# Moving the ordering and turning of the last part of w eleven places later, and regrouping the engines that copy it

## The chip, the cores and the metric

One core of a Trainium2 chip (trn2). The metric is the device time of one execution in microseconds (us), the median of several. The program runs on one core only. Profiles are of single executions; their span is some 1.8 us shorter than the device time of the same execution.

## The reference, cut to what matters

```python
# inputs: r_inputs (B=4096, F=32, D=64) float32, W (P=496, 64, 64) float32, P = F (F-1) / 2
idx_i, idx_j = np.triu_indices(F, k=1)
vi = inputs[:, idx_i, :]
vj = inputs[:, idx_j, :]
vidots = jnp.einsum('bpd,pde->bpe', vi, W)
return vidots * vj                       # (4096, 496, 64) float32: 520 MB
```

Each of 496 pairs of fields has its own 64 x 64 matrix. The output is large (520 MB), the inputs small (42 MB together).

## The kernel before

A tile is 128 rows of the batch; there are 32. A tile takes 46 steps (up to 16 pairs each), in five output parts of 6, 7, 9, 10 and 14 steps; one transfer writes one part of one tile. The first three tiles are interleaved part by part, because w comes in only while they run: part 1 of tiles 0, 1, 2 (steps 0 to 17), part 2 (18 to 38), part 3 (39 to 65), part 4 (66 to 95), part 5. Each part of w (w0 to w3, 128 pairs each, w3 112) is loaded, brought into another order by four copies ("order", `rp<-raw`), turned by TensorE and copied out of PSUM ("turn", `ptw`, `wT`). w2 and w3 share one raw buffer, so w3 can be loaded only when the last copy of w2 has read it.

```python
    tpool = ctx.enter_context(tc.tile_pool(name="tpool", bufs=4))    # rp and tmp share these four
    opool = ctx.enter_context(tc.tile_pool(name="opool", bufs=3))    # output parts
...
        pool, tag = ((opool, "ot"), (opool, "ot"), (const, "w3"), (const, "w3"))[c]
...
    def order_w(c: int, k: int, copy):
        r = wrows[c][1] - wrows[c][0]
        rp = tpool.tile([P, EU, 2, D], F32, tag="tmp", name=f"rp_{c}_{k}")
        src = raw[c][:r, :].rearrange("p (d h e) -> p e h d", h=2, d=D)
        copy(rp[:r], src[:, k * EU : (k + 1) * EU])
        return rp
...
    for c, orders, turns in (                       # at which step of the interleaved schedule
        (1, (2, 4, 8, 10), (4, 7, 12, 15)),
        (2, (17, 22, 27, 32), (19, 24, 29, 34)),
        (3, (43, 44, 45, 46), (48, 50, 52, 54)),
    ):
...
    no_aside = range(41, 55)
...
                rps[c, k] = order_w(c, k, p if c > 1 and k % 2 else v)   # p GpSimd, v VectorE
                if (c, k) == (2, NU - 1):
                    load_w(3, nc.scalar)
...
        if i in aside and c0 == 0 and s not in no_aside:     # "aside": ScalarE and GpSimd
            tmp = tpool.tile([P, CH, 2, E2], F32, tag="tmp", name=f"tmp_{s}")
            nc.scalar.copy(tmp, src)
            nc.gpsimd.tensor_mul(dst, tmp, xj)
        else:
            nc.vector.tensor_mul(dst, src, xj)
```

The order in which an engine runs its instructions is not quite the written one: in the trace of this kernel VectorE's two copies of w3, written for steps 43 and 45, run right after its product of step 39. In the lines of a trace, `ot<-ps,xs` is a product on VectorE, `ot<-tmp,xs` one on GpSimd, `out_dram<-ot` an output.

Of the kernel before, what the change touches and what calls it, by code (L numbers as in the profile page):

```python
# [12 lines left out]
def kernel(  # L13
# [52 lines left out]
    def rows_of(dram: bass.AP, blk: int) -> bass.AP:  # L66
        return dram[blk * NB * P : (blk + 1) * NB * P]

    def new_x(blk: int):

        xs[blk] = xpool.tile([P, 1 + NB * F, D], F32, tag="xs", name=f"xs_{blk}")
        nc.gpsimd.memset(xs[blk][:, 0, :], 0.0)  # L72

    def load_x(blk: int, eng, k0: int = 0, k1: int = NB):
        src = rows_of(x, blk).rearrange("(p k) f d -> p (k f) d", k=NB)
        eng.dma_start(out=xs[blk][:, 1 + k0 * F : 1 + k1 * F, :], in_=src[:, k0 * F : k1 * F, :])  # L76
# [7 lines left out]
    def load_w(c: int, eng=nc.sync):  # L84

        a, b = wrows[c]
        pool, tag = ((opool, "ot"), (opool, "ot"), (const, "w3"), (const, "w3"))[c]
        raw[c] = pool.tile([P, D * D], F32, tag=tag, name=f"raw_{c}")
        eng.dma_start(out=raw[c][: b - a, :], in_=wflat[a:b])
# [8 lines that stand above are left out]
    def turn_w(c: int, k: int, rp, copy):  # L98
        r = wrows[c][1] - wrows[c][0]
        if c not in wT:  # L100
            wT[c] = const.tile([P, r, E2], F32, tag=f"w{c}", name=f"wT_{c}")
        pt = psum.tile([P, EU, P], F32, tag="ps", name=f"ptw_{c}_{k}")
        for n in range(EU):
            nc.tensor.transpose(  # L104
                pt[:, n, :r], rp[:r, n].rearrange("p h d -> p (h d)"), ident[:r, :r]
            )
        copy(wT[c][:, :, k * EU : (k + 1) * EU], pt[:, :, :r].rearrange("p e r -> p r e"))  # L107

    def turn_x(blk: int, k: int, q: int, copy):

        pt = psum.tile([P, RUN, P], F32, tag="ps", name=f"ptx_{blk}_{k}_{q}")
        for n in range(RUN):
            s = k * F + q * RUN + n
            nc.tensor.transpose(  # L114
                pt[:, n, :], xs[blk][:, s : s + 2, :].rearrange("p f d -> p (f d)"), ident
            )
        xT = xtpool.tile([P, RUN, P], F32, tag="xT", name=f"xT_{blk}_{k}_{q}")
        copy(xT, pt)  # L118
        return xT
# [31 lines left out]
    for c, orders, turns in (  # L151
        (1, (2, 4, 8, 10), (4, 7, 12, 15)),
        (2, (17, 22, 27, 32), (19, 24, 29, 34)),
        (3, (43, 44, 45, 46), (48, 50, 52, 54)),
    ):
        for k in range(NU):
            due.setdefault(orders[k], []).append(("order", c, k))
            due.setdefault(turns[k], []).append(("turn", c, k))
    no_aside = range(41, 55)
    LATE = 6  # L160
    loads = {place[blk * NB, LATE]: blk + 1 for blk in range(2, NBLK - 1)}
    loads[place[LEAD, LATE]] = 2
# [10 lines left out]
    v, p, a = nc.vector.tensor_copy, nc.gpsimd.tensor_copy, nc.scalar.copy  # L173
    xT, rps = {}, {}
# [8 lines left out]
    for s, (t, st) in enumerate(sched):  # L183
        blk, kt = divmod(t, NB)
        g, i, c0, m = steps[st]
        if s in loads:
            new_x(loads[s])
            load_x(loads[s], nc.scalar)
        for what, *args in due.get(s, ()):
            if what == "x":  # L190
                xT[tuple(args)] = turn_x(*args, a)
            elif what == "turn":
                turn_w(*args, rps.pop(tuple(args)), a)
            else:
                c, k = args
                rps[c, k] = order_w(c, k, p if c > 1 and k % 2 else v)
                if (c, k) == (2, NU - 1):
                    load_w(3, nc.scalar)

        base, end = groups[g]  # L200
        pa = p0[i] + c0
        if pa == base:
            ots[t] = opool.tile([P, cap, D], F32, tag="ot", name=f"ot_{t}_{g}")
        ot = ots[t]
        ps = psum.tile([P, 2, CH, E2], F32, tag="ps", name=f"ps_{s}")
        for c, (lo, hi) in enumerate(wrows):
            lo, hi = max(pa, lo), min(pa + m, hi)
            if lo < hi:
                for h in range(2):
                    n = i + 1 - h  # L210
                    nc.tensor.matmul(  # L211
                        ps[:, h, lo - pa : hi - pa, :],
                        xT[blk, kt, n // RUN][h * D : (h + 1) * D, n % RUN, :],
                        wT[c][h * D : (h + 1) * D, lo - wrows[c][0] : hi - wrows[c][0], :],
                        start=True,
                        stop=True,
                    )
        o = pa - base
        j = 1 + kt * F + i + 1 + c0
        dst = ot[:, o : o + m, :].rearrange("p m (h e) -> p m h e", h=2)  # L220
        src = ps[:, :, :m, :].rearrange("p h m e -> p m h e")
        xj = xs[blk][:, j : j + m, :].rearrange("p m (h e) -> p m h e", h=2)
        if i in aside and c0 == 0 and s not in no_aside:
# [6 lines that stand above are left out]
        ends = (p0[2], end) if s < NS and (t, g) == (0, 0) else (end,)  # L230
        if pa + m in ends:
            n0 = p0[2] if len(ends) > 1 and pa + m == end else base
            nc.sync.dma_start(  # L233
                out=rows_of(out, blk).rearrange("(p k) n d -> p k n d", k=NB)[:, kt, n0 : pa + m, :],
                in_=ot[:, n0 - base : pa + m - base, :],
            )
# [27 lines left out]
```

## Time and profile before

| | before |
|---|---|
| device time, median of 3 (range) | 1362.47 us (1362.38 to 1362.98) |
| span of the profiled run | 1360.9 us |
| share of the span busy: PE, DVE, ACT, POOL | 87%, 71%, 27%, 39% |
| mean of the transfers over the span | 414 GB/s |
| the same from 80 to 105 us | 281 GB/s |
| the same from 300 to 600 us | 421 GB/s |

Read the last two rows together. In all but its start the kernel moves about 421 GB/s; between 80 and 105 us it moves a third less, and what is not moved there has to be moved later. The lines behind the table are in the prediction.

### The profile page before, as it was taken

What the parts mean: (1) busy time and instruction counts of PE and PEld (TensorE: products, weight loads), DVE (VectorE), ACT (ScalarE), POOL (GpSimd) and SP (SyncE); (2) the same over time, 40 slices, a digit from 0 to 9 for tenths busy, and PEclk for the clock granted to TensorE, in tenths of its full rate; (3) what the DMA queues carried; (4) which work ended last, traced back from release to release, by engine and by line L of the source; (5) the groups of instructions that cost most, each with busy time, mean ns of one, the idle gap of its engine ahead of it and who ended that gap; (6) DMA issues with size and microseconds to landing.
All of it is one profiled execution on the core that took longest, in us unless ns stands there. A gap on an engine that the chain in (4) does not pass through costs nothing.

```text
span 1360.9 us, 17864 instructions
## 1 busy us (share of the span) xinstructions
PE 1178.6 (87%) x7424; PEld 690.8 (51%) x7424; DVE 960.9 (71%) x1263; ACT 371.5 (27%) x366; POOL 534.4 (39%) x247
## 2 busy tenths in 40 slices
PE   6969898889889897988879989898887989988994
PEld 4546554545455454554445555455554545545552
DVE  4778776757777676776767767577775768767774
ACT  3422222222222222322322222222222322223321
POOL 1634233443333443434434334443344434344431
PEclk9989998989989899998989989899998999989997
DMA  9979999999999999999999999999999999999997
GB/s 380 371 320 432 420 428 433 430 426 426 420 415 423 429 416 414 422 416 424 425 412 417 420 415 426 416 419 412 427 410 421 426 413 424 409 431 421 419 419 318
DMA packets 26273, 562.92 MB, mean 414 GB/s; under 512 B 2912, under 2 KB 2912, under 8 KB 3040
## 3 DMA queue, kind: packets, MB, share of 16 engines
q1 hardware_dynamic: 24048, 530.59, 91.9%
q10 hardware_dynamic: 2144, 31.20, 5.5%
q8 instruction: 58, 0.95, 0.3%
q14 instruction: 23, 0.19, 0.0%
HBM read 41.68 MB, written 520.09 MB: 413 GB/s over the span
## 4 chain that ended last, share of the span: by engine, by line
DMA 49%; PE 27%; DVE 17%; POOL 2%; issue 2%; ACT 0%; DVEq 0%; SPq 0%; POOLq 0%; ACTq 0%
DMA out_dram<-ot 47%; PE ps L211 22%; DVE ot L228 17%; PE ptx L114 4%; POOL ot L226 2%; DMA raw<-in_L_rec_W_dram 2%; PE ptw L104 1%; DVE rp L95 0%; ACT tmp L225 0%; POOL rp L95 0%; DVEq L228 0%; ACT wT L107 0%; SPq L76 0%; SPq L233 0%; POOLq L226 0%
## 5 line engine op out<-in xcount | busy, mean ns | idle before, releaser
L228 DVE TENSOR_TENSOR ot<-ps,xs 128x1024 f32<-128x1024 f32 (+15 forms) x1251 | 945.2, 809 | 361.0 <-DMA out_dram<-ot 179.5
L211 PE MATMUL ps<-wT,xT 64*128 64x512 f32 (+13 forms) x6272 | 1033.7, 473 | 131.6 <-DVE ot L228 120.3
L211 PEld LDWEIGHTS ps<-wT,xT 64*128 64x128 f32 x6272 | 563.8, 197 | 566.6 <-DVE ot L228 305.3
L226 POOL TENSOR_TENSOR ot<-tmp,xs 128x1024 f32<-128x1024 f32 x221 | 522.2, 2363 | 644.5 <-ACT tmp L225 456.3
L225 ACT COPY tmp<-ps 128x1024 f32<-128x1024 f32 x221 | 223.9, 1013 | 505.6 <-PE ps L211 462.2
L118 ACT COPY xT<-ptx 128x1024 f32<-128x1024 f32 x128 | 129.6, 1013 | 440.2 <-PE ptx L114 440.2
L114 PE MATMUL ptx<-ident,xs 128*128 128x128 f32 x1024 | 141.2, 281 | 28.9 <-DVE ot L228 20.1
L114 PEld LDWEIGHTS ptx<-ident,xs 128*128 128x128 f32 x1024 | 111.0, 142 | 74.5 <-issue 44.3
L72 POOL MEMSET xs<- 128x64 f32 x16 | 2.4, 152 | 148.2 <-DVE ot L228 148.2
L95 DVE COPY rp<-raw 128x1024 f32<-128x1024 f32 (+1 forms) x11 | 15.1, 1410 | 18.1 <-DMA raw<-in_L_rec_W_dram 18.1
L104 PE MATMUL ptw<-ident,rp 128*128 128x128 f32 (+1 forms) x128 | 18.9, 303 | 3.9 <-DVE rp L95 3.9
L104 PEld LDWEIGHTS ptw<-ident,rp 128*128 128x128 f32 (+1 forms) x128 | 16.1, 158 | 11.0 <-DVE rp L95 5.0
L107 ACT COPY wT<-ptw 128x1024 f32<-128x1024 f32 (+1 forms) x15 | 14.8, 985 | 17.6 <-PE ptw L104 15.2
L95 POOL COPY rp<-raw 128x1024 f32<-128x1024 f32 (+1 forms) x4 | 9.4, 2350 | 6.7 <-DMA raw<-in_L_rec_W_dram 6.7
L107 DVE COPY wT<-ptw 128x1024 f32<-128x1024 f32 x1 | 1.2, 1225 | 3.5 <-PE ptw L104 3.5
L95 ACT COPY rp<-raw 128x1024 f32<-128x1024 f32 x1 | 2.0, 1964 | 1.8 <-DMA raw<-in_L_rec_W_dram 1.8
L118 ACT ACT_TABLE_LOAD x1 | 1.3, 1283 | 0.7 <-PEq L251 0.7
masks.py:197 POOL MEMSET ident<- 128x128 f32 x1 | 0.2, 205 | 0.3 <-POOLq L251 0.3
masks.py:199 POOL TENSOR_SCALAR_AFFINE_SELECT ident<-ident 128x128 f32<-128x128 f32 x1 | 0.3, 294 | 0.0
L251 POOL MEMSET const-float32-0.0<- 128x1 f32 x1 | 0.1, 99 | 0.2 <-issue 0.2
L251 POOL MEMSET const-bfloat16-1.0<- 128x1 bf16 x1 | 0.1, 102 | 0.0
L251 POOL MEMSET const-uint8-127<- 128x1 uint8 x1 | 0.1, 102 | 0.0
(1 smaller groups left out, 0.1 us busy)
## 6 DMA issues: line engine op xcount, KB each, us to landing
out_dram<-ot SPq DMA_DIRECT2D x64, 3360.0 KB, 16.2
out_dram<-ot SPq DMA_DIRECT2D x32, 3168.0 KB, 15.2
out_dram<-ot SPq DMA_DIRECT2D x32, 3104.0 KB, 17.0
out_dram<-ot SPq DMA_DIRECT2D x31, 2880.0 KB, 16.4
xs<-in_r_inputs_dram ACTq DMA_DIRECT2D x14, 2048.0 KB, 16.6
raw<-in_L_rec_W_dram SPq DMA_DIRECT2D x3, 2048.0 KB, 14.5
xs<-in_r_inputs_dram SPq DMA_DIRECT2D x2, 1024.0 KB, 11.1
xs<-in_r_inputs_dram SPq DMA_DIRECT2D x1, 2048.0 KB, 24.9
```

The lines of the kernel that those rows point to most:

```text
L72: nc.gpsimd.memset(xs[blk][:, 0, :], 0.0)
L95: copy(rp[:r], src[:, k * EU : (k + 1) * EU])
L104: nc.tensor.transpose(pt[:, n, :r], rp[:r, n].rearrange("p h d -> p (h d)"), ident[:r, :r])
L107: copy(wT[c][:, :, k * EU : (k + 1) * EU], pt[:, :, :r].rearrange("p e r -> p r e"))
L114: nc.tensor.transpose(pt[:, n, :], xs[blk][:, s : s + 2, :].rearrange("p f d -> p (f d)"), ident)
L118: copy(xT, pt)
L211: nc.tensor.matmul(ps[:, h, lo - pa : hi - pa, :], xT[blk, kt, n // RUN][h * D : (h + 1) * D, n % RUN, :], wT[c][h * D : (h + 1) * D, lo - ...
L225: nc.scalar.copy(tmp, src)
L226: nc.gpsimd.tensor_mul(dst, tmp, xj)
L228: nc.vector.tensor_mul(dst, src, xj)
L251: nc = _bacc.Bacc("TRN2", target_bir_lowering=False, num_devices=1)
```

## The change

Its intent: w3 is needed for the first time at step 75, but its ordering stood at step 43, where VectorE and GpSimd met a load that had not landed. The ordering and turning go eleven places later, and half of w3's copies go from GpSimd to ScalarE. The new expression also sends w2's two even copies from VectorE to GpSimd.

```diff
-        (3, (43, 44, 45, 46), (48, 50, 52, 54)),
+        (3, (54, 54, 55, 55), (57, 60, 63, 66)),
...
-    no_aside = range(41, 55)
+    no_aside = range(52, 67)
...
-                rps[c, k] = order_w(c, k, p if c > 1 and k % 2 else v)
+                rps[c, k] = order_w(c, k, (v, v, p, v)[c] if k % 2 == 0 else (v, v, p, a)[c])
```

## The prediction

> **What bounds the kernel now.** I read the page first (which engine is full, and where in the span), then the chain of waits around the odd slice, then a table of windows cut at the edges that the chain gave, then each engine's timeline there.
>
> The page: the DMA row gives the busy share of the 16 engines in each fortieth of the span (34 us), GB/s what they moved.
>
> ```profile
> span 1360.9 us, 17864 instructions
> ...
> DMA  9979999999999999999999999999999999999997
> GB/s 380 371 320 432 420 428 433 430 426 426 420 415 423 429 416 414 422 416 424 425 412 417 420 415 426 416 419 412 427 410 421 426 413 424 409 431 421 419 419 318
> ```
>
> The transfers are full from the fourth slice on, at about 420 GB/s; the kernel is bound by writing its 520 MB. Only the first three slices and the last are below that. So the change can earn nothing but DMA idle time in the start, and the third slice (68 to 102 us, 320 GB/s) is the worst. The chain of waits between 40 and 130 us (start, length, what):
>
> ```profile
> 51.63 2.41 POOL ot L226
> 54.05 1.94 POOL rp L95
> 55.98 0.02 issue
> 56.01 16.33 DMA raw<-in_L_rec_W_dram
> ...
> 73.37 5.04 DVE rp L95
> 78.41 0.61 DVE ot L228
> 79.02 0.04 issue
> 79.06 1.97 PE ptx L114 x8
> ```
>
> The last part of w (w3) can be loaded only when GpSimd's last ordering copy of w2 has left the shared buffer (55.98); it lands at 72.34; then VectorE copies it for six microseconds; then TensorE goes on. Windows (time, length, busy time per engine, PE clock, DMA share, GB/s):
>
> ```profile
> 65.80:80.20 14.40, 2.92 (x22) 2.21 (x19) 7.77 (x5) 0.33 (x1) 7.68 (x3) 0.73 1.00 425
> 80.20:84.90 4.70, 4.70 (x28) 3.23 (x28) 3.78 (x5) 1.44 (x2) 0.04 (x1) 0.74 0.02 3
> 84.90:92.90 8.00, 8.00 (x64) 5.60 (x62) 5.75 (x6) 3.40 (x5) 0.00 (x0) 1.00 0.95 406
> 92.90:95.60 2.70, 2.70 (x22) 1.55 (x20) 2.20 (x4) 0.74 (x2) 0.00 (x0) 1.00 0.00 0
> 80.00:105.00 25.00, 25.00 (x177) 16.36 (x175) 19.13 (x26) 10.47 (x11) 7.33 (x4) 0.95 0.66 281
> 300.00:600.00 300.00, 266.87 (x1682) 155.36 (x1680) 216.40 (x287) 81.96 (x81) 121.59 (x55) 0.95 0.99 421
> ```
>
> While the engines stand still the DMA still has work, until 80.2; then it is idle for 4.7 us, writes one output, and is idle again for 2.7 us. The output issues in SyncE's timeline agree: none between 65.81 and 84.94, the next at 95.61. The engines' timelines of the copies concerned, VectorE's, GpSimd's and ScalarE's (start, length, instructions merged, idle time before and what ended it):
>
> ```profile
> 50.77 1.05 DVE L95 COPY rp<-raw 128x1024 f32<-128x1024 f32 x1
> 62.87 2.75 DVE L228 TENSOR_TENSOR ot<-ps,xs 128x640 f32<-128x640 f32 x3 [1.19 <-PE ps L211]
> 72.43 5.98 DVE L95 COPY rp<-raw 112x1024 f32<-112x1024 f32 x2 [6.81 <-DMA raw<-in_L_rec_W_dram]
> ```
>
> ```profile
> 72.46 2.77 POOL L95 COPY rp<-raw 112x1024 f32<-112x1024 f32 x1 [6.67 <-DMA raw<-in_L_rec_W_dram]
> ```
>
> ```profile
> 11.31 1.96 ACT L95 COPY rp<-raw 128x1024 f32<-128x1024 f32 x1 [1.78 <-DMA raw<-in_L_rec_W_dram]
> ```
>
> An ordering copy costs VectorE 1.05 us alone, but 2.99 each (5.98 for two) beside a copy on GpSimd; GpSimd 1.99 alone (at 42.20 and 53.99) and 2.7 here; ScalarE 1.96. VectorE's 6.81 us of waiting and 5.98 of copying are the hole in which no product was written out.
>
> **What the Trainium skill says.** "SBUF — State Buffer", section "SBUF: two separate sides": VectorE in a two-port mode and GpSimd take an exclusive lock on a shared port pair for a whole instruction; ScalarE has ports of its own. The 5.98 us for two copies against 2 x 1.05 agrees in direction. "ScalarE: Activation LUTs", section "What ACT_TABLE_LOAD costs": an activation with immediate scale and bias takes 186 ns + 0.833 ns per element, 1.04 us for 1024. The copies out of PSUM agree (1013 ns); the strided ordering copy took 1.96, and I use that. "DMA: Bandwidth & Descriptors", section "Issuing engines are not separate DMA queues": transfers issued from different engines interleave on the same 16 engines. The w3 load agrees: 1.79 MB took 16.33 us beside the outputs, 110 GB/s of the 425 moved. So an earlier order to read w3 is not to be had cheaply, a later use is.
>
> **The change part by part.** Steps 39 to 65 of the interleaved schedule are the third of five output parts for tiles 0, 1, 2 (nine steps each); step 66 on is the fourth part.
>
> First, the four w3 orderings leave steps 43 to 46 for 54 and 55, and the turns leave 48 to 54 for 57 to 66. The turned w3 holds pairs from 384 on and is first read at step 75 (the tenth step of the fourth part), so nothing waits for it that did not. Removed from VectorE at 65.6 us: 6.81 + 5.98 = 12.8 us. TensorE stood from 67.6 (four PSUM buffers full) to 79.06: 11.5 us. That is the most the engines can gain.
>
> What the DMA makes of it: between 80 and 105 us it moved 281 x 25 = 7.0 MB. At the 421 GB/s of the full stages that is 16.7 us. So 8.3 us is to be had: 4.7 + 2.7 idle, and the rest because a transfer alone in the queue ran at 406. It is had in full if the third part's outputs are issued before the queue runs dry. Estimate: tile 0 has about 40 matmuls at 6.43/40 us (the 40 before the hole) = 6.4 us and one turn of x (1.0): issued at about 65.8 + 7.4 = 73.2. Tile 1 carries two ordering copies on VectorE and one product more: seven products outside the aside 5.5 us (from the means by form), + 1.2 + 2 x 1.05 = 8.8: 82. Tile 2 has all nine products on VectorE, 8.0: 90. The queue, at 3.24 MB per output and 421 GB/s (7.7 us), would be empty at 80.2, 87.9, 95.6. Margins of 7, 6 and 6 us: no idle. Gain 8.3.
>
> Second, half of the w3 copies go to ScalarE: 2 x 1.96 us on an engine that is 27% busy, and VectorE's two return from 2.99 to about 1.05. This lies inside the margin.
>
> Third, and not in the words of the change: the new expression sends all four w2 copies to GpSimd; two of them (steps 17 and 27) were VectorE's. GpSimd gets 2 x 1.99 = 4.0 us, VectorE loses 2.1, which earns nothing as TensorE is 100% busy from 20 to 66 us. GpSimd was idle 3.6 us before 39.52 and 1.6 us before 48.15, which would take most of it. What doesn't fit pushes the aside products, the w3 load and the outputs of the second part. Estimated cost 0 to 2.4 us; I take 0.7.
>
> Fourth, the steps that may not use the aside become 52 to 66 instead of 41 to 54: four products instead of three are moved to VectorE, +1.2 us, counted above.
>
> Sum: 1362.5 - 8.3 + 0.7 = 1354.9, say 1355.
>
> **Rivals.** (a) The wait stays in another place: the copies run in an order near, but not equal to, the written one (the w3 copies of step 43 ran right after the product of step 39). If VectorE still meets them before the load lands, only their cost shrinks, and the hole ends about 4 us earlier: 1358. Eleven places are about 8 us of work, and the load was 6.8 late, so this is close, but the 6 us margin covers a small rest. ScalarE, too, may now stand before w3 and hold up turns of x. (b) GpSimd becomes the bound from 40 to 62 us, being busy 13.7 of 18 us from 38 to 56: everything 2.4 us later or more, 1357 to 1358. (c) The transfers hide it all: 1362. Against it: from 130 us on the queue is never empty, so idle time in the start is never made good, and its removal is passed on in full. (d) The engines' whole 11.5 us is won: 1351. Against it: the queue has no more than 8.3 to give here.
>
> **Range and chances.** The centre is 1355; a full gain with no loss on GpSimd, or a little DMA idle before 56 us saved too, gives 1353; (a) and (b) together about 1360. I put 8 in 10 between 1353 and 1360. Two per cent is 27 us, three times all the idle at issue, so within 2% is nearly certain: faster 0.01, same 0.98, slower 0.01.
>
> **What would show it.** Right: the third slice rises from 320 towards 420 GB/s, no window of DMA share 0 between 80 and 96, the first output of the third part issued at 72 to 78 instead of 84.94, the VectorE copies of w3 near 1.05 us, the span shorter by the DMA idle removed, and slices four to 39 unchanged. Wrong: outputs of the second part issued over 2 us later (then the GpSimd term is too small), a new wait of ScalarE or VectorE for the load of w3 that outlasts the queue, or the same hole at another place.

## The result, and the profile after

| | before | changed |
|---|---|---|
| device time, median (range) | 1362.62 us (1362.38 to 1362.98), 4 runs | 1355.01 us (1354.39 to 1355.39), 4 runs |
| ratio, 95% interval | | 0.9943 (0.9926 to 0.9961) |
| span of the profiled run | 1360.9 us | 1353.3 us |
| transfers, 80 to 105 us | 281 GB/s | 402 GB/s |
| outputs of part 3 issued, tiles 0, 1, 2 | 84.94, 95.61, 101.68 us | 71.24, 85.44, 94.85 us |

A ratio is the mean time of one kernel's fast runs over that of the other's of the same rounds, so it is not quite the ratio of the medians. The change makes the kernel 7.6 us faster by the medians, which is 0.6% and well within 2%.

The page of the changed kernel: the span, the transfers' busy share and what they moved, in fortieths of the span.

```profile
span 1353.3 us, 17856 instructions
...
DMA  9999999999999999999999999999999999999997
GB/s 386 370 426 408 424 427 431 428 432 431 418 414 419 433 412 418 422 413 426 428 407 422 417 425 410 423 421 407 425 410 426 419 422 427 401 432 428 415 417 319
```

The third slice went from 320 to 426 GB/s, and its busy digit from 7 to 9. The second slice (370) is still low. The fourth fell from 432 to 408 (the low share near 103 us, shown below, lies in it); those after it are about as before. So the time was won in the third slice.

The chain of waits of the changed kernel, from 56 us on:

```profile
56.12 2.42 POOL ot L226
58.54 0.02 issue
58.55 16.29 DMA out_dram<-ot
...
75.64 2.61 DVE rp L95
78.25 0.60 DVE ot L228
78.85 0.95 DVE rp L95
```

The load of w3 is gone from it. At the same place there is now a transfer in the other direction: the output issued at 58.55 (part 2 of tile 1), whose buffer part 3 of tile 1 needs. It is split into sixteen shares; the first landed at 72.75 us, the last at 74.84, and VectorE began at 74.96. VectorE's timeline there, then ScalarE's and GpSimd's:

```profile
69.55 1.62 DVE L228 TENSOR_TENSOR ot<-ps,xs 128x1024 f32<-128x1024 f32 x2 [0.30 <-PE ps L211]
74.96 0.76 DVE L228 TENSOR_TENSOR ot<-ps,xs 128x576 f32<-128x576 f32 x1 [3.79 <-DMA out_dram<-ot]
75.64 2.61 DVE L95 COPY rp<-raw 112x1024 f32<-112x1024 f32 x1
78.16 0.69 DVE L228 TENSOR_TENSOR ot<-ps,xs 128x512 f32<-128x512 f32 x1
78.76 1.04 DVE L95 COPY rp<-raw 112x1024 f32<-112x1024 f32 x1
```

```profile
72.13 1.93 ACT L95 COPY rp<-raw 112x1024 f32<-112x1024 f32 x1
77.38 1.98 ACT L95 COPY rp<-raw 112x1024 f32<-112x1024 f32 x1 [3.33 <-POOL ot L226]
```

```profile
75.00 2.35 POOL L226 TENSOR_TENSOR ot<-tmp,xs 128x1024 f32<-128x1024 f32 x1 [4.40 <-DMA out_dram<-ot]
```

Three things are to be seen. VectorE waits 3.79 us, no longer for w3 but for the output buffer. Its two copies took 2.61 and 1.04 us: the first began at 75.64, while GpSimd was in a product from 75.00 to 77.35, and ended 0.9 us after that product. This is what the Trainium skill, "SBUF — State Buffer", section "SBUF: two separate sides", describes: the shared port pair is held for a whole instruction, and the other engine waits until it is free. The trace fits: elsewhere in this trace VectorE's ordering copies take 1.02 to 1.07 us, and 77.35 + 1.05 = 78.40, 0.15 us from the measured end. And ScalarE's second copy waited 3.33 us for GpSimd's product, which by the program still held the last of the four shared `tmp` buffers.

The kernel before shows the same. The line of 5.98 us for two copies in the prediction merges one of 1.03 us and one of 5.04. Here are that second copy of VectorE and the product that GpSimd ran right behind its own copy (72.46 to 75.23):

```profile
73.37 5.04 DVE L95 COPY rp<-raw 112x1024 f32<-112x1024 f32 x1
75.19 2.34 POOL L226 TENSOR_TENSOR ot<-tmp,xs 128x1024 f32<-128x1024 f32 x1
```

The copy ended at 78.41, 0.88 us after that product (77.53): it outlasted a copy and a product of GpSimd, not a copy alone.

The windows of the changed kernel (time, length, busy time of PE, PEld, DVE, ACT and POOL, PE clock, DMA share, GB/s):

```profile
80.00:93.00 13.00, 12.88 (x79) 8.41 (x79) 10.61 (x13) 3.73 (x4) 0.00 (x0) 0.80 1.00 431
93.00:96.00 3.00, 3.00 (x26) 1.98 (x24) 2.17 (x3) 0.91 (x1) 0.00 (x0) 1.00 0.91 377
96.00:102.00 6.00, 5.95 (x46) 3.81 (x44) 4.68 (x8) 2.02 (x2) 1.93 (x1) 1.00 0.94 401
102.00:104.00 2.00, 2.00 (x16) 0.91 (x12) 2.00 (x4) 1.01 (x1) 0.53 (x2) 1.00 0.57 241
80.00:105.00 25.00, 24.83 (x165) 15.96 (x163) 20.46 (x27) 7.67 (x8) 3.46 (x2) 0.90 0.94 402
```

The gaps of 4.7 and 2.7 us are gone, but not everything: near 103 us the share falls to 0.57. In bytes, (402 - 281) x 25 us = 3.0 MB more were moved in this stretch, which at 421 GB/s is 7.2 us; the time fell by 7.6.

### The profile page after: what moved, and what is told of

It reads as the page before. It is cut to its first block, busy times and chain, and to the rows that moved or that the text cites. A ratio compares the mean times of both kernels' runs of the same rounds, so it can differ in the third digit from the quotient of the medians.

```text
span 1353.3 us, 17856 instructions
## 1 busy us (share of the span) xinstructions
PE 1180.3 (87%) x7424; PEld 690.9 (51%) x7424; DVE 956.9 (71%) x1262; ACT 374.1 (28%) x367; POOL 530.2 (39%) x246
## 4 chain that ended last, share of the span: by engine, by line
DMA 50%; PE 25%; DVE 17%; POOL 3%; issue 2%; ACT 0%; DVEq 0%; SPq 0%; POOLq 0%; ACTq 0%
DMA out_dram<-ot 50%; PE ps L211 20%; DVE ot L228 17%; PE ptx L114 4%; POOL ot L226 3%; PE ptw L104 1%; DMA raw<-in_L_rec_W_dram 1%; ACT tmp L225 0%; DVE rp L95 0%; POOL rp L95 0%; DVEq L228 0%; ACT wT L107 0%; SPq L76 0%; POOLq L226 0%; SPq L233 0%
## 5 line engine op out<-in xcount | busy, mean ns | idle before, releaser
L95 DVE COPY rp<-raw 128x1024 f32<-128x1024 f32 (+1 forms) x9 | 10.7, 1219 | 11.1 <-DMA raw<-in_L_rec_W_dram 11.1
L95 POOL COPY rp<-raw 128x1024 f32<-128x1024 f32 x4 | 8.0, 1994 | 0.1
L95 ACT COPY rp<-raw 112x1024 f32<-112x1024 f32 (+1 forms) x3 | 5.9, 1959 | 5.1 <-POOL ot L226 3.3
```

## The experiments

All are correct in their results. Each batch had its own runs of the kernel before: medians 1362.86 (first four), 1362.54 (next four), 1362.55 us (last two), 9 runs each.

**Theory.** The time is lost exactly where the queue of transfers runs dry in the start; what the engines wait for matters only where it makes the queue run dry. **Rivals.** The copies' cost on GpSimd and VectorE was what counted, not their place; GpSimd's additional copies of w2 cost something that a better version would win back; the wait for the load merely sits somewhere else; and the many later transfers hide any wait in the start.

### The places alone

```diff
-(v, v, p, v)[c] if k % 2 == 0 else (v, v, p, a)[c]
+p if c > 1 and k % 2 else v
```

> Only the places move (orders 54/55, turns 57 to 66); the engines of the copies are those of before: w2 half on VectorE, w3 half on GpSimd. My theory (the gain is DMA idle time taken away by using w3 later): nearly all of it stays, 1355 to 1357 us; two VectorE copies of about 3 us each beside GpSimd make the third part's second output up to 2.4 us later, which the queue just about covers. Rival (the gain is the copies leaving GpSimd, which had slowed VectorE): little stays, 1360 to 1362.

Measured: 1356.04 us (1355.01 to 1356.74, 5 runs), ratio 0.9949 (0.9936 to 0.9961). VectorE's two copies took 5.23 us together, because GpSimd made a product and a copy at the same time (74.18 to 79.2 us); the second output of part 3 went out at 86.35. The place alone brings 6.8 us (1362.86 - 1356.04) of the 7.6 to 7.8 that the whole change brings. The missing 0.8 to 1.0 us fits the engines' part, but the ranges of this kernel and of the changed one overlap (1355.01 to 1355.39), so it is not settled by the times alone. The places here include the range of steps that may not use the aside, which returns steps 44 and 49 to ScalarE and GpSimd; that range was not varied alone.

### The engines alone

```diff
-        (3, (54, 54, 55, 55), (57, 60, 63, 66)),
+        (3, (43, 44, 45, 46), (48, 50, 52, 54)),
-    no_aside = range(52, 67)
+    no_aside = range(41, 55)
```

> Only the engines change (w3 half on ScalarE, all of w2 on GpSimd); the places are those of before, 43 to 46. My theory: VectorE still stands before w3 until it lands (about 72.5), but its copies cost 1.05 instead of 2.99 us, so the hole ends about 4 us earlier, the first DMA gap (4.7) shrinks to about 1 and the second (2.7) stays: about 1358.6 us, half of the gain. Rival (engines are all of it): 1355. Rival (places are all of it): 1362.

Measured: 1357.99 us (1356.25 to 1358.47), ratio 0.9962 (0.9949 to 0.9974). VectorE's timeline of this run:

```profile
71.23 1.03 DVE L95 COPY rp<-raw 112x1024 f32<-112x1024 f32 x1 [5.67 <-DMA raw<-in_L_rec_W_dram]
72.18 0.69 DVE L228 TENSOR_TENSOR ot<-ps,xs 128x512 f32<-128x512 f32 x1
72.78 1.03 DVE L95 COPY rp<-raw 112x1024 f32<-112x1024 f32 x1
```

The wait for w3 is all there (5.67 us), yet almost two thirds of the gain are too. Without GpSimd beside it VectorE copies in 1.03 us, the first output of part 3 goes out at 79.45 instead of 84.94, just before the queue would be dry, and only a gap from 88 to 91 us, ahead of the second (issued at 90.79), is left; 80 to 105 us moved 374 GB/s. The two halves of the change bring 4.9 and 6.8 us alone and about 7.7 together: they do not add up, since both fill the same gap in the queue.

### w2 back on VectorE

```diff
-(v, v, p, v)[c] if k % 2 == 0 else (v, v, p, a)[c]
+(v, v, v, v)[c] if k % 2 == 0 else (v, v, p, a)[c]
```

> The changed kernel with w2's two copies back on VectorE; w3 half on ScalarE as changed. The prediction's third term (all of w2 on GpSimd costs 0.7 us, range 0 to 2.4): this kernel is 0.7 faster than the changed one, 1354.3. Rival, which the trace of the changed kernel suggests (the copies went into GpSimd's idle gaps, w3's load was issued 0.2 us later only): no difference, 1355.0 +- 0.3.

Measured: 1355.11 us (1354.58 to 1355.52), ratio 0.9942. The same as the changed kernel. With all of w2 on GpSimd no output of part 2 was issued more than 0.3 us later than in the kernel before. (Counted from each execution's first output, the second one was 0.7 us later and the third level.) GpSimd's timeline in the changed kernel shows the two added copies:

```profile
35.44 1.97 POOL L95 COPY rp<-raw 128x1024 f32<-128x1024 f32 x1
...
49.93 2.00 POOL L95 COPY rp<-raw 128x1024 f32<-128x1024 f32 x1
```

The first of them lies in the 3.6 us that the prediction had found idle before 39.52. The second follows the product that it has to let pass, and pushes the next one by less than a microsecond. The load of w3 is issued at 56.22 us in the changed kernel and at 55.62 with w2 back on VectorE, and that costs nothing: it lands at 70.22, and VectorE is not free before 71.2.

### The w3 copies ahead of the buffer wait

```diff
-        (3, (54, 54, 55, 55), (57, 60, 63, 66)),
+        (3, (51, 51, 52, 52), (57, 60, 63, 66)),
-    no_aside = range(52, 67)
+    no_aside = range(49, 67)
```

> The changed kernel with the w3 orders at 51, 51, 52, 52 (no aside from 49), which puts VectorE's two copies four products earlier, ahead of the end of tile 0's third part. In the changed kernel VectorE waited 3.8 us for an output buffer (71.2 to 75.0) and made the copies after it, and the queue ran dry for about 1 us near 103. Theory (the buffer wait plus copies after it cost the rest): the copies now lie before the buffer comes free, the third part's second output is issued near 82.5 instead of 85.4, no gap near 95 or 103, 1353.8 us. Rival (the load of w3, landing near 70.2, is met too early and the wait comes back): 1356 or more.

Measured: 1354.58 us (1354.1 to 1355.1), ratio 0.9939 (0.9926 to 0.9951). The step worked as meant: the copies took 1.97 us together and ended before the buffer came free, the second output went out at 82.55, and no gap was left. VectorE's timeline and the windows of this run:

```profile
70.71 1.97 DVE L95 COPY rp<-raw 112x1024 f32<-112x1024 f32 x2 [3.06 <-DMA raw<-in_L_rec_W_dram]
```

```profile
93.00:96.00 3.00, 2.89 (x22) 1.93 (x22) 2.16 (x5) 1.61 (x2) 0.00 (x0) 1.00 1.03 436
96.00:102.00 6.00, 6.00 (x45) 3.67 (x44) 5.32 (x7) 1.81 (x3) 4.04 (x2) 1.00 0.98 422
102.00:104.00 2.00, 2.00 (x18) 1.22 (x16) 0.53 (x2) 1.63 (x2) 0.92 (x2) 1.00 1.02 439
80.00:105.00 25.00, 24.89 (x180) 15.60 (x178) 20.17 (x28) 9.11 (x10) 5.96 (x3) 1.00 1.00 429
```

VectorE waits again for the load (3.06 us), and that costs nothing, as the queue still holds work. But the gain is 0.2 to 0.5 us by the medians (against the two measurements of the changed kernel and the kernel with w2 back), where 27 GB/s x 25 us = 0.7 MB more, 1.6 us at 421 GB/s, had been moved by 105 us. The expectation was missed here: an emptier gap did not give its whole length back.

The landings tell where it went. The trace keeps sixteen landing events for each transfer, one for each of its sixteen shares. In this table (worked out from them) are the issue of an output, and the landing of its first and of its last share, in us:

```
                          changed kernel             copies ahead of the buffer wait
                          issued  first   last       issued  first   last
part 3, tile 1             85.44   94.98   97.13      82.55   94.90   97.02
part 4, tile 0            103.63  112.83  113.12     100.09  110.31  113.17
part 4, tile 1            110.91  120.84  122.88     107.38  118.26  121.46
part 5, tile 0            126.06  136.87  138.96     122.53  134.14  139.79
part 5, tile 1            135.22  150.29  151.70     131.69  146.93  151.18
first tile after these    158.09  172.44  174.04     157.92  169.08  173.95
```

In parts 4 and 5 the outputs are issued 3.5 us earlier and their first shares land 2.5 to 3.4 us earlier. Their last shares, with which the buffer comes free, are 1.4 us earlier once (part 4, tile 1), but 0.8 us later soon after and about half a microsecond earlier at 151; at 174 us they are level. The sixteen shares have drifted apart (139.79 - 134.14 = 5.7 us against 2.1). So the additional bytes were moved by the shares that were ahead.

That lead does not last: this run had moved 416 GB/s against 411 in the changed kernel over the first 250 us, but 417 against 416 over the first 400. By then both kernels are in the same condition. Of an output issued at 364 us fifteen shares had landed by 379.28 us in the changed kernel and by 379.16 here, and the sixteenth landed at 383.66 and at 383.52. In every kernel, the one before included, the last share landed 3.3 to 5.4 us after the fifteenth for outputs issued between 350 and 400 us. So filling the gap let fifteen shares reach sooner a lead that they reach in any case. That this lead is all that ate the gain is argued from these landings, not tested; which share is the slow one, whether it is always the same, and why it is slower can't be told from these traces and stays open.

### Later still

```diff
-        (3, (54, 54, 55, 55), (57, 60, 63, 66)),
+        (3, (60, 60, 61, 61), (63, 66, 69, 72)),
-    no_aside = range(52, 67)
+    no_aside = range(58, 73)
```

> The changed kernel with everything of w3 six places later still: orders 60, 60, 61, 61, turns 63, 66, 69, 72, no aside from 58 to 72 (first use of w3 stays at 75). Theory (only an empty transfer queue costs, and the wait for the load is already gone at 54): 1354.5 to 1355.5, no further gain. Rival (the later the better, because part of the wait for w3 is still in the changed kernel): 1353.5 or less.

Measured: 1354.60 us (1353.75 to 1355.23), ratio 0.9940 (0.9928 to 0.9952). No further gain beyond the spread. The place is a plateau from 51 to 60, not a slope.

### First part written in more pieces

```diff
-        ends = (p0[2], end) if s < NS and (t, g) == (0, 0) else (end,)
+        ends = (p0[2], end) if t < LEAD and g == 0 else (end,)
```

(with the orders at 51 and 52)

> The kernel with the orders at 51 and 52, and besides the first output part of tiles 1 and 2 is written in two pieces, as tile 0's is already, so that the queue is fed sooner between 26 and 38 us, where it moved 341 GB/s (full stages: 421; (421-341) x 12 / 421 = 2.3 us). The prediction's rule that idle time removed in the start is passed on in full: 1352.3. Rival (the run with the orders at 51 and 52 removed all idle after 65 us and gained only 0.4, so the rule does not hold for the last microseconds, something else sets the pace from about 150 us on): 1354 to 1354.6.

Measured: 1354.51 us (1353.14 to 1354.86), ratio 0.9938 (0.9925 to 0.9952). The time is what the rival said, but the run doesn't test it: the first piece of tile 1 went out at 35.89, the second at 36.32, so the cut fed the queue no sooner, and the window from 26 to 38 us stayed at 332 GB/s. The first piece holds a product that GpSimd finishes late. The cut was mended below.

### The load of w3 held back, twice

```diff
+        if s == 44:      # second kernel: 39
+            hold = const.tile([P, D * D], F32, tag="w3", name="hold")
+            nc.scalar.copy(hold[:, :8], ps[:, 0, 0, :8])
+            load_w(3, nc.scalar)
...
-                if (c, k) == (2, NU - 1):
-                    load_w(3, nc.scalar)
```

> The changed kernel with the load of w3 held back on purpose: its buffer is first written by an eight-column copy of the products of step 44, so the load is issued near 69.5 instead of 56.2 us and lands near 84. Theory (time is lost exactly as far as the wait outlasts the queue): VectorE and ScalarE wait for the load to 84, the second output of the third part is issued near 92.7 instead of 85.4, the queue is dry for 4 to 6 us, 1359 to 1361. Rival (the wait is hidden by the many later outputs): 1355.

> The same as the run before with the copy after step 39, the load issued near 65.5 us and landing near 79.5. Theory: VectorE waits some 4 us more than in the changed kernel, but the second output of the third part goes out near 88, about when the queue runs dry, so almost nothing is lost: 1355 to 1356.3. Rival (each microsecond of waiting for w3 costs one): 1358 to 1359.

Measured after step 44: 1362.27 us (1361.5 to 1362.74), ratio 0.9996 (0.9983 to 1.0008). The whole gain is gone, with the copies where the change put them. VectorE's timeline and the windows of this run:

```profile
85.25 1.04 DVE L95 COPY rp<-raw 112x1024 f32<-112x1024 f32 x1 [14.02 <-DMA raw<-in_L_rec_W_dram]
```

```profile
80.00:93.00 13.00, 5.93 (x32) 4.34 (x34) 7.48 (x9) 5.26 (x4) 0.00 (x0) 0.59 0.52 217
...
80.00:105.00 25.00, 17.88 (x118) 12.16 (x120) 17.73 (x22) 8.74 (x8) 0.00 (x0) 0.79 0.69 291
```

The load was issued at 66.72 and landed at 84.76; the second output of part 3 went out at 93.03 and the third at 101.70, and before each the queue ran dry. The time is 1.3 us above the expected range; the expectation had named a dry queue before the second output only, and not the second gap, before 101.70.

Measured after step 39: 1356.28 us (1355.01 to 1357.39), ratio 0.9953 (0.9941 to 0.9966). The load landed at 79.26, VectorE waited 7.25 us for it, and the second output went out at 87.17, against 85.44 in the changed kernel. Of these 7.25 us of waiting for w3 some 1.3 us came through to the time (1356.28 - 1355.01, with ranges that overlap). They are not all additional: the changed kernel's 3.79 us of waiting for the output buffer are gone here, so VectorE waited 3.5 us more in all. Together the two runs answer the rival that the start is hidden, and the rival that each microsecond of waiting counts: neither holds; what counts is the time for which the queue is dry.

### The changed kernel again, and a better cut

The second of these has the orders at 51 and 52, and a cut of the first part after 31 pairs in tiles 1 and 2:

```diff
-        ends = (p0[2], end) if s < NS and (t, g) == (0, 0) else (end,)
+        cut = p0[2] if t == 0 else p0[1]
+        ends = (cut, end) if t < LEAD and g == 0 else (end,)
...
-            n0 = p0[2] if len(ends) > 1 and pa + m == end else base
+            n0 = cut if len(ends) > 1 and pa + m == end else base
```

> The changed kernel itself once more, beside the next run on the same chip, since its four runs and those of the later variants lie within half a microsecond: 1355.0 +- 0.4.

> The kernel with the orders at 51 and 52, and the first part of tiles 1 and 2 written in two pieces cut after 31 pairs (the cut of the run before came with the rest, 0.4 us apart, and fed nothing sooner). The first 31 pairs of tile 1 come from VectorE alone and can go out near 31.5 instead of 35.9 us. Rule of the prediction (idle removed in the start is passed on in full): the 26 to 38 us window rises from 341 to about 390 GB/s, 1.4 us saved, 1353.1. Rival (another pace-setter from 150 us on, so the last microsecond is not passed on): the window rises the same, the time stays at 1354.2 to 1354.8.

Measured: the changed kernel 1354.80 us (1354.43 to 1355.23), ratio 0.9942 (0.9928 to 0.9955); the one with the cut 1353.95 us (1353.38 to 1354.51), ratio 0.9936 (0.9924 to 0.9949). The first piece of tile 1 now goes out at 31.29, and 26 to 38 us moved 375 instead of 332 GB/s. In the 18 us after that, 372 instead of 399 were moved, so of 1.2 us gained ((375 - 332) x 12 / 421) about 1.2 ((399 - 372) x 18 / 421) were given back at once: TensorE was busy there for 18.00 of the 18 us and could not supply more. What is left is 0.85 us by the medians, between the two expectations, with ranges that overlap a little. It is not the cut's alone, as the orders are at 51 and 52 as well; against the kernel with these orders and no such cut (1354.58) it is 0.63. It is the fastest kernel, by a margin that these runs don't quite prove.

### All of them in one line

With r the GB/s moved between 80 and 105 us in the profiled run, the estimate is 1362.6 - (r - 281) x 25 / 421:

| kernel | r | estimate, us | measured median, us |
|---|---|---|---|
| before | 281 | | 1362.6 |
| load held back to step 44 | 291 | 1362.0 | 1362.3 |
| engines alone | 374 | 1357.1 | 1358.0 |
| places alone | 390 | 1356.1 | 1356.0 |
| load held back to step 39 | 392 | 1356.0 | 1356.3 |
| w2 back on VectorE | 401 | 1355.5 | 1355.1 |
| changed | 402 | 1355.4 | 1355.0 |
| first part in more pieces | 422 | 1354.2 | 1354.5 |
| changed, again | 423 | 1354.2 | 1354.8 |
| orders at 60 and 61 | 428 | 1353.9 | 1354.6 |
| orders at 51 and 52 | 429 | 1353.8 | 1354.6 |
| the better cut | 431 | 1353.7 | 1354.0 |

The estimate is within a microsecond of the medians over the whole range, whatever made the queue run dry, and it is 0.3 to 0.8 us too low at its lower end. (r is from one execution, the median from several. Against that same execution's own time the estimate is off by up to 1.3 us: the profiled one with the orders at 51 and 52 took 1355.10. The executions also differ from their start on: the first output left between 26.16 and 27.46 us.) The changed kernel appears twice, with 402 and 423 GB/s and almost the same time, which shows that the last 20 GB/s of this stretch are worth little.

## Why the prediction was right or wrong

The time was right: 1355.0 predicted, 1355.01 measured. Two terms of its sum were mis-sized in opposite directions, and the agreement to a hundredth is chance.

- **What bounds the kernel, and that only idle time of the transfers in the start can be won:** right. The third slice rose from 320 to 426 GB/s, the fourth fell from 432 to 408, the later ones stayed, and holding the load back gave the whole gain back (1362.27).
- **The gain of 8.3 us, "Margins of 7, 6 and 6 us: no idle":** too large by about 1 us. By the bytes 7.2 us were won in that stretch. The first margin held (issued at 71.24, estimated 73.2). The second output went out at 85.44, not 82, because part 3 of tile 1 had to wait 3.79 us for an output buffer, which the estimate never asked about, and because the first copy took 2.61 us instead of 1.05: 71.24 + 8.8 (its own sum for tile 1) + 3.79 + 1.56 = 85.39. Some 1 us of low share near 103 us was left. Taking that away (orders at 51 and 52) gave 0.2 to 0.5 us.
- **"VectorE's two return from 2.99 to about 1.05":** half right. The second took 1.04; the first ran into a product on GpSimd. The reading under it was wrong: 2.99 is the mean of 1.03 and 5.04, and what the 5.04 waited for was a copy and a product of GpSimd. I had taken the copies away from GpSimd but not counted its products.
- **The copies on ScalarE:** right, 1.93 and 1.98 us against 1.96, inside the margin, with a wait of 3.33 us for the shared `tmp` buffers in between.
- **GpSimd's four copies of w2, 0.7 us:** too large. With the two added ones taken back the time is the same (1355.11), so the term is zero within about 0.3 us. The first idle spell that the prediction named took one of the copies; the other ran at 49.93, after the spell that it named, and pushed little. A slip without effect: 1792 KB of 1024 bytes are 1.84 MB, so the load of w3 ran at 112 GB/s and not at 110.
- **"idle time in the start is never made good, and its removal is passed on in full":** right for the large gaps, as the table above shows, wrong for the last microsecond, where most shares of the transfers got ahead and the last share soon landed no earlier.
- **Rival (a), the wait staying in another place:** its size was well put for the engines alone (it said 1358 for that case; measured 1357.99). In the changed kernel itself the load had landed (70.22) before VectorE came to it; ScalarE did stand, but before `tmp` and not before w3. **Rival (b)**, GpSimd as the bound, did not come. **Rival (d)** was rightly put aside: no kernel reached 1351.

## What to carry to other kernels

When the transfers bound a kernel, a wait of the engines costs only the time for which it leaves the queue empty; so set each engine wait against the time at which the queued outputs run out, not against the length of the wait. When a wait is taken away, ask of the next instruction what else it needs (here the output buffer, and the port that a product on GpSimd holds), because that wait comes next. And the last microsecond of an idle gap may not be passed on: here an output freed its buffer only when the slowest of its shares had landed. Last, look at single instructions before taking a mean: a merged line can hide one of 1.03 and one of 5.04 us.

## What the Trainium skill lacked or had wrong

- "ScalarE: Activation LUTs", section "What ACT_TABLE_LOAD costs": the rule of 186 ns + 0.833 ns per element gives, as an estimate, 1.04 us for 1024 elements. The copies out of PSUM took 1.01 us, but the ordering copies, which read SBUF with a large stride, took 1.93 to 1.99 us over all runs, almost double. That section has no word on strided reads. "SBUF — State Buffer" does say that each access that crosses to a new 16-byte line pays a penalty, but not how large it is for ScalarE. No run here has a ScalarE copy from SBUF without the stride, so that the stride is the cause is not shown.
- "DMA: Bandwidth & Descriptors": section "Queues, rings and completion order" says that one copy is split across up to sixteen rings, and a table of the page that two of the DMA engines are usually slower in traces, but no figure is given for how far the shares drift apart. In the changed kernel the first and the last share of an output landed 2.1 us apart near 97 us and 5.8 us apart near 390 us, most of it by one share alone.
- No page says how far the place where an instruction is written can be from the place where it runs. VectorE's copies written for steps 43 and 45 ran right after its product of step 39; in the run with the orders at 51 and 52 they ran ahead of the product of step 45, and in the changed kernel the one of step 54 ran ahead of the product of step 50 and the one of step 55 right after it.
